# Two graph-attention layers on one core: h0's first pieces on POOL's queue, PSUM release by tile, another order at layer 2's opening and at its end

## The chip, the cores and the metric

The kernel runs on 1 core of one Trainium2 chip. The metric is the device time of that core in microseconds, the median of several runs. The core's engines are named as in the profile: PE (matrix products and transposes; PEld is its loading of weights), DVE and ACT (vector and scalar work), POOL (GpSimd, which here issues the gathers) and SP (which here issues plain loads and stores). SP, ACT and POOL each have a queue of DMA instructions that stands in the same row as the engine's other work; the transfers themselves run on the core's 16 DMA engines.

## The reference

A graph of 3125 nodes with 768 features has 53,125 edges, sorted by their destination: 25,000 random pairs in both directions and one loop for each node. The layer is two graph attentions with residual products:

```
h  = relu(layernorm(x))
h0 = h
h  = gat(h, W1, a_src1, a_dst1, b1, heads=4, out=256, concat)      # 1024 wide
h  = relu(layer_norm(h, g1, be1)) + (h0 @ Wr1 + br1)
h1 = h
h  = gat(h, W2, a_src2, a_dst2, b2, heads=1, out=768)
h  = layer_norm(h, g2, be2) + (h1 @ Wr2 + br2)
return x + h

gat: xl = x @ W
     e = leaky_relu(<xl[src], a_src> + <xl[dst], a_dst>, 0.2)
     alpha = exp(e - max over the edges of dst) / (sum over the edges of dst + 1e-16)
     out[dst] = sum over the edges of alpha * xl[src] + bias
```

Everything is float32.

## The kernel before

The nodes are cut into 25 blocks of 128 (the last, block 24, has 53). A block's edges lie in up to 17 tiles of 128 slots (8 in the last block), which are treated in five rounds (`ROUNDS`). Each tile is one gather: an indirect DMA on POOL's queue (lines 210 and 214) that reads 128 rows of a table in memory into a buffer `g`. PE then multiplies each gathered tile with a small matrix of weights into the block's accumulator `pa` in PSUM (line 782 in layer 1, 1437 in layer 2).

The stages follow each other in time. Up to about 300 us the kernel makes layer 1's table `h @ W1` and the lists of edges. From 300 to 490 us it looks up the scores of all edges and makes their weights `al`; beside this, `early` multiplies the first three groups of `h0` (`h0g`) with `Wr1` (line 1035, 24 products a group, each read out by ACT at line 1038 into `rt`). From 490 to 1183 us `sums` runs layer 1's gathers. It has 16 gather buffers, g0 to g15. Beside the sums, `later` makes the residual products that are left: it loads pieces of h0 (`h0k`, 11 buffers, line 1133), multiplies them into `pr` (line 190) and has ACT read them out (line 1157). The generator `first` calls `totals` once at the beginning: PE transposes the weights (line 599, tile `p` with the tag `p2`), ACT copies them out (line 601), DVE scans them into sums for each node (line 666), PE transposes back (line 610), SP stores the result `alo_d` (line 671), and POOL then looks up each block's own row of it (`ao`, line 724). At the end of each block `end1` does the layer norm, transposes, adds the residual, and multiplies with W2 into layer 2's table.

From 1183 us layer 2 runs: a ring of 36 gather buffers, the softmax of the edges of each block (`softmax`, in two parts of five transposes `mix` each, with DVE and ACT between), `summed` (the products into `pa`), `residuals` (a generator of 8 steps for each block, two products `pr` from a piece of h1 and `Wr2` each, called by `filled(n)`; after the 8th, DVE adds `pr` to `xr`, line 1329), and `finish` (own row, bias, layer norm, residual, store). While block b is summed, the softmax of block b + 1 is made. `STEPS` says how many residual steps follow each round, and `REST` how many come at a block's end:

```
AHEAD = 3
STEPS = [0, 1, 1, 0, 4]
REST = 2
```

The order on PE, ACT and DVE from 490 us on is that of the program's text (`tc.manual_schedule`); POOL and SP are ordered by the framework's scheduler. A pool of tiles gives its memory or its PSUM banks on in one of two ways: with `reuse_waits="tile"` a new tile waits for the readers of what lay in its own place, without it for the earlier pool as a whole. DMAs take their semaphores from two sets of eight, one for SP and ACT together and one for POOL; in a set, each DMA waits for the one that stood eight before it.

`own` is a block's own row of the table, which SP loads (line 227); `slots` holds the edge scores that `values` copies out of the gathered rows on ACT (line 1376); `load_own`, `own_share` and `store_rows` are helpers for the own row's load, its scaling with the share of the loop (on POOL, for the last block alone), and the store of the result. The source also has a second program for edges in any order, which does not run on this input.

Of the kernel before, what the change touches and what calls it, by code (L numbers as in the profile page):

```python
# [10 lines left out]
F32 = mybir.dt.float32  # L11
# [6 lines left out]
OP = mybir.AluOpType  # L18
AX = mybir.AxisListType
PSUM = bass.MemoryType.PSUM  # L20
# [49 lines left out]
def in_order(  # L70
# [16 lines left out]
    nc = tc.nc  # L87
# [4 lines left out]
    C2 = W2.shape[1]  # L92
    P = 128
# [132 lines left out]
        for o, e in pieces(b):  # L226
            q.dma_start(t[o:e], src_[b * P + o:b * P + e, :])

    def store_rows(q, dst_, b, t):
        for o, e in pieces(b):  # L230
            q.dma_start(dst_[b * P + o:b * P + e, :], t[o:e])

    def by_chunk(vec, pool, n, name):

# [564 lines left out]
    with tc.tile_pool(name="m1", bufs=1) as mp:  # L799
# [323 lines left out]

        with tc.tile_pool(name="w2", bufs=1, reuse_waits="tile") as wp, tc.tile_pool(name="e1", bufs=2, reuse_waits="tile") as ep, \
                tc.tile_pool(name="a1", bufs=1, reuse_waits="tile") as ap, \
                tc.tile_pool(name="g1", bufs=1, reuse_waits="tile") as gp, tc.tile_pool(name="pg1", bufs=1, space=PSUM) as pp:
            loaded, made, whole, gone = {}, {}, set(), set()

            def load(i, k, q=nc.sync):
                if i < NG:  # L1130
                    n = cols_of(i)
                    t = loaded[i, k] = wp.tile([128, WIDE], F32, name="h0k", bufs=11)
                    q.dma_start(t[:, :n], h0T_d[i][:, k, :n])

            for k in range(NK1):
                load(0, k, nc.scalar)
            b1_b = wp.tile([P, HC], F32, name="b1_b")
            nc.sync.dma_start(b1_b, bcast(b1, HC))
            def later():
# [102 lines left out]
    with tc.tile_pool(name="m2", bufs=1, reuse_waits="tile") as mp, \  # L1242
# [66 lines left out]
        def halves(t):  # L1309

            return t.rearrange("p (i n) -> p i n", i=2)
# [27 lines left out]
        def filled(n):  # L1339
            for _ in range(n):  # L1340
                next(fill, None)
# [24 lines left out]
        def load_own(b, cs=slice(0, C2)):  # L1366
            if b < NB:
                if b == NB - 1 and b not in owns:
                    owns[b] = small([128, NK2, P], "h1", bufs=3).rearrange("p k n -> p (k n)")[:, :C2]
                own = owns[b] = owns.get(b) or small([128, C2], "own")  # L1370
                load_rows(nc.sync, own[:, cs], table2[:, cs], b)
# [15 lines left out]
        def softmax(b):  # L1387

            nonlocal e0, w0
            at, pen = slots[b % 2], pens.pop(b)  # L1390
            mix = pp.tile([128, 1024], F32, name="mix")
            for c in range(WIN // 128):
                o = FROM[c % 4] + c // 4
                nc.tensor.transpose(mix[:, c * 128:(c + 1) * 128], at[:, o:o + 4].rearrange("p q n -> p (q n)"), ident)  # L1394
            top = small([P, 1], "top", bufs=2)
            e, e0 = e0 or small([P, WIN], "e"), None
            sums_ = mix[:, :WIN]
            nc.vector.tensor_tensor_reduce(out=sums_, in0=sums_, in1=pen, scale=1.0, scalar=-BIG,
                                           op0=OP.add, op1=OP.max, accum_out=top)
            nc.vector.tensor_scalar(top, top, both[:, b:b + 1], -1.0, op0=OP.max, op1=OP.mult)  # L1400
            nc.vector.scalar_tensor_tensor(top, top, SLOPE, top, op0=OP.mult, op1=OP.min)
            nc.scalar.activation(e, sums_, AF.Copy, scale=SLOPE)
            nc.vector.tensor_tensor(e, sums_, e, OP.max)
            v = small([P, 4], "v", bufs=3)
            nc.scalar.activation(e, e, AF.Exp, bias=top, accum_out=v[:, 0:1])
            nc.scalar.activation(v[:, 1:2], self_s[:, b:b + 1], AF.Exp, bias=top)
            penalty(b + 1)
            yield
            for c in range(WIN // 128):
                nc.tensor.transpose(mix[:, c * 128:(c + 1) * 128], e[:, c * 128:(c + 1) * 128], ident)  # L1410
            yield
            w, w0 = w0 or small([128, WIN], "w", bufs=2), None
            nc.vector.tensor_copy(w[:, :512], mix[:, :512])
            nc.scalar.activation(w[:, 512:], mix[:, 512:WIN], AF.Copy)
            shares[b] = w, v
# [26 lines left out]
        def finish(b, pa):  # L1442

            nonlocal z0
            r = rows_of(b)
            own, v = owns.pop(b), shares.pop(b)[1][:r]
            z, z0 = (z0 or small([P, C2], "z", bufs=2))[:r], None
            if b < NB - 1:
                p = pa[:, :, :f]
                nc.vector.scalar_tensor_tensor(p, halves(own), v[:, 2:3], p, op0=OP.mult, op1=OP.add)  # L1450
                yield
                nc.vector.scalar_tensor_tensor(p, p, v[:, 3:4], halves(b2_b), op0=OP.mult, op1=OP.add)
                yield from norm_steps(mp, p, C2, 1)
                mu, rstd = norm_steps.found
                nc.vector.scalar_tensor_tensor(p, p, mu, halves(g2_b), op0=OP.subtract, op1=OP.mult)
                nc.vector.scalar_tensor_tensor(halves(z), p, rstd, halves(xrs.pop(b)), op0=OP.mult, op1=OP.add)
            else:
                for i in range(2):
                    cs = slice(i * f, (i + 1) * f)
                    nc.vector.scalar_tensor_tensor(z[:, cs], pa[half_at(b, i), i, :f], v[:, 3:4], own[:r, cs],  # L1460
                                                   op0=OP.mult, op1=OP.add)
                yield
                yield from norm_steps(mp, z, C2, 1)
                mu, rstd = norm_steps.found
                nc.vector.scalar_tensor_tensor(z, z, mu, g2_b[:r], op0=OP.subtract, op1=OP.mult)
                nc.vector.scalar_tensor_tensor(z, z, rstd, xrs.pop(b)[:r], op0=OP.mult, op1=OP.add)
            store_rows(nc.scalar, out, b, z)

        def totals2(b):
            v = shares[b][1][:rows_of(b)]  # L1470
# [4 lines left out]
        def own_share(b):  # L1475
            r = rows_of(b)
            own, v = owns[b][:r], shares[b][1][:r]
            nc.gpsimd.tensor_scalar(own, own, v[:, 2:3], v[:, 3:4], op0=OP.mult, op1=OP.mult)
            nc.gpsimd.tensor_tensor(own, own, b2_b[:r], OP.add)

        with tc.manual_schedule(engines={PE, ACT, DVE}):
            penalty(0)
            fetch()
            load_own(0)
            filled(AHEAD * NK2)
            for k in range(len(ROUNDS)):
                values(0, k)
            made = softmax(0)
            next(made)
            filled(NK2 // 2)  # L1490
            next(made)
            next(made, None)
            totals2(0)
            values(1, 0)
            values(1, 1)
            ending = iter(())
            for b in range(NB):
                pa = pp.tile([P, 2, 512], F32, name="pa", bufs=2)
                opened = set()
                last = b + 1 == NB - 1  # L1500
                steps = STEPS if b else [0] * (len(ROUNDS) - 1) + [NK2 // 2 - REST]
                for k in range(len(ROUNDS)):
                    if last and k == 0:
                        load_own(b + 1)
                        for i in range(2, len(ROUNDS)):
                            values(b + 1, i)
                        made = softmax(b + 1)
                        next(made)
                    summed(b, k, pa, opened)
                    if k < 2:  # L1510
                        next(ending, None)
                        if 0 < b < NB - 1:
                            load_own(b, slice(k * f, (k + 1) * f))
                    if b + 1 < NB and not last:
                        if k < 3:
                            values(b + 1, k + 2)
                        if k == 2:
                            made = softmax(b + 1)
                            next(made)
                    if k == 2:  # L1520
                        for _ in ending:
                            pass
                    if k == 4:
                        ending = finish(b, pa)
                        next(ending)
                    if k == 4:
                        filled(steps[k])
                    if b + 1 < NB and k == (1 if last else 4):
                        next(made)
                        next(made, None)  # L1530
                        totals2(b + 1)
                        if last:
                            own_share(b + 1)
                    filled(REST if k == 4 else steps[k])
                if b + 2 < NB:
                    values(b + 2, 0)
                    values(b + 2, 1)
            for _ in ending:
                pass
# [472 lines left out]
```

## Time and profile before

| | |
|---|---|
| time, median of 3 runs | 1728.88 us (1728.3 to 1729.52) |
| the profiled execution | 1734.45 us, span 1732.3 us, mean granted clock 0.980 |
| busy share of the span | PE 94%, PEld 54%, DVE 58%, ACT 26%, POOL 50% |
| DMA | 546.69 MB, mean 316 GB/s |
| 0 to 300 us (table 1, lists) | PE busy 287.76 us, DMA share 0.55 |
| 300 to 490 us (weights of the edges) | PE busy 187.53 us, DMA share 0.44 |
| 490 to 1183 us (layer 1's sums) | PE busy 674.61 us, DMA share 0.98 |
| 1183 to 1732 us (layer 2) | PE busy 479.11 us, DMA share 0.98 |

The span is the stretch in which the profiled execution has records; its own time is 2.15 us longer. In a timeline, a row holds the start in us, the busy time, the engine ("ACTq" and "SPq" are DMA issues on those queues), the line, the operation, its output and inputs, the number of instructions, and in brackets the idle time ahead of it with what ended it. In a row of grouped instructions the count is followed by the busy time, the mean ns of one, and the idle time ahead of the group with its releasers. A DMA share of 1 means that all 16 engines are busy; it can read a little over 1.

### The profile page before, as it was taken

The numbers are of one execution on the slowest core, as the hardware profiler recorded it, in microseconds if no ns is written. First come the engines' busy times: TensorE is split into PE (matmuls) and PEld (weight loads), VectorE is DVE, ScalarE is ACT, GpSimd is POOL, SyncE is SP. The second block draws the span as 40 slices with busy tenths as digits, with TensorE's granted clock in tenths as the row PEclk, the third lists the DMA queues.
The fourth block names the chain that finished last, engine by engine and source line by source line (L and its number), as shares of the span: only waits on it lengthen the run. The fifth ranks groups of instructions, "written<-read, shape, count | busy, mean of one in ns | idle before, by whom it ended". The sixth has DMA issues, their size and how long they took to land.

```text
span 1732.3 us, 31368 instructions
## 1 busy us (share of the span) xinstructions
PE 1629.0 (94%) x11522; PEld 934.1 (54%) x11522; DVE 1004.0 (58%) x2604; ACT 456.0 (26%) x1312; POOL 871.9 (50%) x909
## 2 busy tenths in 40 slices
PE   7999999999979999999999999998799999998985
PEld 5666666566646556565565555544444444444431
DVE  6784343799963665565655656751344544444455
ACT  2122333100122122121221212112334444434443
POOL 2000010200055766667667666745777677777772
PEclk9999999999989999999999999999899999999997
DMA  6843546743189999999999999987999999999994
GB/s 225 278 135 117 144 119 183 275 141 121 45 300 346 408 403 396 404 395 404 406 391 408 387 378 384 410 340 276 385 378 396 378 395 396 393 397 396 380 350 161
DMA packets 188212, 546.69 MB, mean 316 GB/s; under 512 B 32072, under 2 KB 80072, under 8 KB 187922
## 3 DMA queue, kind: packets, MB, share of 16 engines
q0 software_dynamic: 99776, 387.46, 58.3%
q1 hardware_dynamic: 83880, 146.74, 24.3%
q10 hardware_dynamic: 4394, 10.39, 1.6%
q8 instruction: 94, 1.54, 0.4%
q14 instruction: 68, 0.56, 0.1%
HBM read 492.19 MB, written 65.62 MB: 322 GB/s over the span
## 4 chain that ended last, share of the span: by engine, by line
PE 69%; DMA 19%; DVE 7%; ACT 2%; issue 2%; SPq 1%; POOL 1%; POOLq 0%; ACTq 0%; DVEq 0%
PE pr L190 15%; PE p L190 14%; PE pm L190 13%; PE pa L782 11%; DMA g<-table,hi_s 6%; DMA g<-table,idx_s 6%; PE pa L1437 4%; PE pm L1035 4%; PE pq L580 3%; DMA h<-h1T_d 2%; DMA s<-slo_d 1%; PE mix L1394 1%; PE p L1200 1%; DMA xr<-in_x_dram 1%; DVE ab L504 1%
## 5 line engine op out<-in xcount | busy, mean ns | idle before, releaser
L210 POOL DMA_INDIRECT g<-table,idx_s x393 | 377.8, 961 | 324.4 <-DVE al L624 160.5
L214 POOL DMA_INDIRECT g<-table,hi_s x423 | 433.8, 1026 | 209.5 <-issue 92.9
L190 PE MATMUL pr<-wr,h 128*128 128x384 f32 x768 | 276.3, 506 | 7.8 <-issue 4.2
L190 PE MATMUL p<-w,h1T 128*128 128x384 f32 (+1 forms) x768 | 267.7, 496 | 0.0
L782 PE MATMUL pa<-g,w 128*32 128x256 f32 x3912 | 244.0, 383 | 7.9 <-DMA g<-table,hi_s 4.7
L190 PEld LDWEIGHTS pr<-wr,h 128*128 128x128 f32 x768 | 143.4, 196 | 117.7 <-issue 41.2
L190 PEld LDWEIGHTS p<-w,h1T 128*128 128x128 f32 x768 | 139.8, 189 | 113.0 <-issue 21.0
L782 PEld LDWEIGHTS pa<-g,w 128*32 128x32 f32 x3912 | 119.5, 110 | 125.8 <-issue 25.2
L1437 PE MATMUL pa<-g,w 128*32 128x384 f32 x1956 | 179.2, 505 | 0.8 <-DVE v L1471 0.8
L759 DVE TENSOR_TENSOR w<-oh,al 128x128 f32<-128x128 f32 (+1 forms) x416 | 132.0, 317 | 53.4 <-PE pa L782 28.7
L190 PE MATMUL pr<-h0k,wr 128*128 128x256 f32 (+1 forms) x576 | 143.2, 395 | 3.6 <-DMA h0k<-h0T_d 3.6
L190 PE MATMUL pm<-w,h0l 128*128 128x344 f32 x432 | 131.3, 459 | 2.0 <-ACT h0l L868 2.0
L190 PE MATMUL pm<-w,h0g 128*128 128x344 f32 x432 | 131.0, 458 | 0.3 <-ACT h0g L868 0.3
L1035 PE MATMUL pm<-h0g,wr 128*128 128x512 f32 x288 | 130.4, 599 | 0.0
L190 PEld LDWEIGHTS pr<-h0k,wr 128*128 128x128 f32 x576 | 106.2, 191 | 34.7 <-issue 11.1
L965 POOL DMA_DIRECT2D hot_d<-ohd x25 | 13.4, 535 | 213.1 <-DVE own L531 123.4
L1437 PEld LDWEIGHTS pa<-g,w 128*32 128x32 f32 x1956 | 58.1, 113 | 112.2 <-issue 97.8
L758 DVE TENSOR_SCALAR oh<-iota_f,rel_s 128x32 f32<-128x32 f32 (+1 forms) x416 | 113.1, 272 | 2.8 <-issue 2.7
L190 PEld LDWEIGHTS pm<-w,h0l 128*128 128x128 f32 x432 | 81.3, 192 | 42.3 <-ACT h0l L868 2.6
L190 PEld LDWEIGHTS pm<-w,h0g 128*128 128x128 f32 x432 | 81.3, 192 | 39.9 <-issue 1.2
L1233 DVE COPY asad<-p 128x2 f32<-128x2 f32 (+1 forms) x25 | 4.0, 159 | 155.2 <-ACT row L1231 155.2
L520 ACT ACTIVATE bn_sd<-bn_mv,eps 128x1 f32<-128x1 f32 (+1 forms) x50 | 14.7, 295 | 274.5 <-DVE bn_mv L516 269.7
(295 smaller groups left out, 1751.4 us busy)
## 6 DMA issues: line engine op xcount, KB each, us to landing
s<-slo_d SPq DMA_DIRECT2D x25, 544.0 KB
table<-row SPq DMA_DIRECT2D x24, 512.0 KB
own<-table SPq DMA_DIRECT2D x24, 512.0 KB
h1T_d<-h1T SPq DMA_DIRECT2D x24, 512.0 KB
h<-h1T_d SPq DMA_DIRECT2D x84, 128.0 KB
table<-row SPq DMA_DIRECT2D x24, 392.0 KB
ring<-in_x_dram SPq DMA_DIRECT2D x24, 384.0 KB
out_dram<-z ACTq DMA_DIRECT2D x24, 384.0 KB
```

What stands on the lines that cost most here:

```text
L190: nc.tensor.matmul(out_, lhsT, rhs, start=start, stop=stop)
L210: nc.gpsimd.indirect_dma_start(out=g, out_offset=None, in_=table[:, :], in_offset=bass.IndirectOffsetOnAxis(ap=idx_s[:, c], axis=0))
L214: nc.gpsimd.indirect_dma_start(out=g, out_offset=None, in_=table[:, :], in_offset=bass.IndirectOffsetOnAxis(ap=idx_k[:, c], axis=0), bound ...
L504: nc.vector.scalar_tensor_tensor(abs_[2 + m][:, cs], w[:, k, cs], 1.0, abs_[m][:, cs], op0=OP.mult, op1=OP.mult, accum_out=to[:, k, m * he ...
L580: nc.tensor.matmul(q[:, j], oh[:P, o:o + 128], tabs[:, i], start=(i == 0), stop=(i == 2))
L758: nc.vector.tensor_scalar(oh, iota_f[:, lo:hi], rel_s[:, c:c + 1], None, op0=OP.is_equal)
L759: nc.vector.tensor_tensor(w, oh[:, None, :].to_broadcast([128, heads, hi - lo]), al[:, POS[j], :, b:b + 1].to_broadcast([128, heads, hi - ...
L782: nc.tensor.matmul(pa[p0:p0 + 32, o // f, o % f:o % f + n], w[:, o // cols, :], g[:, o:o + n], start=to not in opened, stop=False, skip_gr ...
L1035: nc.tensor.matmul(pm, wr1[:, k, m * 128:(m + 1) * 128], groups[gi][:, k, :], start=(k == 0), stop=(k == NK1 - 1))
L1200: nc.tensor.transpose(pt[:, k, :r], z[:, (k0 + k) * 128:(k0 + k + 1) * 128], ident[:r, :r])
L1394: nc.tensor.transpose(mix[:, c * 128:(c + 1) * 128], at[:, o:o + 4].rearrange("p q n -> p (q n)"), ident)
L1437: nc.tensor.matmul(pa[p0:p0 + 32, i, :f], w_, g[:, i * f:(i + 1) * f], start=(i, q) not in opened, stop=False, skip_group_check=True)
```

## The change

There are five edits.

1. The first six pieces of h0 that `later` uses (`load(0, k, ...)`) are issued by POOL, where ACT issued them.
2. The PSUM pool of layer 1's sums (`pg1`) hands its banks on by tile, and two tiles, named `pr` and `p2`, are made first, so that these names get the first banks and `pa` the last four.
3. At layer 2's opening 23 residual steps are made instead of 24, then the whole softmax of block 0 without steps inside (before, four steps stood between its parts), then one step. Block 0 gets the same steps as the other blocks (8, where it had 4).
4. For block 23, the last full one, POOL scales the own row and adds the bias (`own_share(b)` after round 1), so that `finish` has one DVE operation ahead of the layer norm where it had two.
5. A block's store that is in pieces has its pieces after the first issued by SP; only the last block's store has a second piece (5 rows).

```
-    def store_rows(q, dst_, b, t):
+    def store_rows(q, dst_, b, t, q1=None):
         for o, e in pieces(b):
-            q.dma_start(dst_[b * P + o:b * P + e, :], t[o:e])
+            (q1 if q1 and o else q).dma_start(dst_[b * P + o:b * P + e, :], t[o:e])
...
-                ... tc.tile_pool(name="pg1", bufs=1, space=PSUM) as pp:
+                ... tc.tile_pool(name="pg1", bufs=1, space=PSUM, reuse_waits="tile") as pp:
...
+            for name in ("pr", "p2"):
+                pp.tile([128, 512], F32, name=name, bufs=2)
             for k in range(NK1):
-                load(0, k, nc.scalar)
+                load(0, k, nc.gpsimd)
...
-            if b < NB - 1:
+            if b == NB - 2:
+                p = pa[:, :, :f]
+                nc.vector.scalar_tensor_tensor(p, p, v[:, 3:4], halves(own), op0=OP.mult, op1=OP.add)
+                yield
+                yield from norm_steps(mp, p, C2, 1)
+                ...
+            elif b < NB - 1:
                 p = pa[:, :, :f]
                 nc.vector.scalar_tensor_tensor(p, halves(own), v[:, 2:3], p, op0=OP.mult, op1=OP.add)
                 yield
...
-            store_rows(nc.scalar, out, b, z)
+            store_rows(nc.scalar, out, b, z, nc.sync)
...
-            filled(AHEAD * NK2)
+            filled(AHEAD * NK2 - 1)
             for k in range(len(ROUNDS)):
                 values(0, k)
-            made = softmax(0)
-            next(made)
-            filled(NK2 // 2)
-            next(made)
-            next(made, None)
+            for _ in softmax(0):
+                pass
+            filled(1)
             totals2(0)
...
-                steps = STEPS if b else [0] * (len(ROUNDS) - 1) + [NK2 // 2 - REST]
...
+                        if last and k == 1:
+                            own_share(b)
...
-                        filled(steps[k])
+                        filled(STEPS[k])
...
-                    filled(REST if k == 4 else steps[k])
+                    filled(REST if k == 4 else STEPS[k])
```

On POOL's queue, where layer 1's first gathers start (`idx_s` holds the edges' row numbers; the names in brackets are the semaphores that a row waits for, DMASW1 being POOL's own set's second one, PE_49 a count of PE's), this stood before:

```order
L210 DMA g_4429<-table_64,idx_s 128x1024 [waits DMASW0_49]
L210 DMA g_4430<-table_64,idx_s 128x1024 [waits DMASW1_49]
L210 DMA g_4431<-table_64,idx_s 128x1024 [waits DMASW2_49]
L210 DMA g_4432<-table_64,idx_s 128x1024 [waits DMASW3_49]
L210 DMA g_4433<-table_64,idx_s 128x1024 [waits DMAHW4_49,DMAHW3_49,DMAHW7_49,DMASW4_49,Activation_49]
```

and this stands now:

```order
L210 DMA g_4431<-table_64,idx_s 128x1024 [waits DMASW0_49]
L1133 DMA h0k<-h0T_d 128x256 [waits DMASW1_49,PE_49]
L1133 DMA h0k<-h0T_d 128x256 [waits DMASW2_49,PE_49]
L1133 DMA h0k<-h0T_d 128x256 [waits DMASW3_49]
L1133 DMA h0k<-h0T_d 128x256 [waits DMASW4_49]
L1133 DMA h0k<-h0T_d 128x256 [waits DMASW5_49]
L1133 DMA h0k<-h0T_d 128x256 [waits DMASW6_49]
L210 DMA g_4432<-table_64,idx_s 128x1024 [waits DMASW7_49]
```

The six loads come after the fourth gather, and seven of the eleven gathers that stood in one row now stand behind them; the first two loads wait for a count of PE's. On ACT's queue the same place (the last copies of the weights' stage, then the copies of `totals`) held the loads before:

```order
L658 ACTIVATE scr<-eo 128x17x100
L1038 ACTIVATE rt<-pm,br_c 128x4x128
L1133 DMA h0k<-h0T_d 128x256 x6
L601 ACTIVATE scr<-p_4501 100x512
L601 ACTIVATE scr<-p_4507 100x512
L601 ACTIVATE scr<-p_4544 100x512
```

and no longer does:

```order
L658 ACTIVATE scr<-eo 128x17x100
L1038 ACTIVATE rt<-pm,br_c 128x4x128
L601 ACTIVATE scr<-p_4503 100x512
L601 ACTIVATE scr<-p_4509 100x512
L601 ACTIVATE scr<-p_4546 100x512
```

The copies follow the last read of `rt` directly. On PE, at layer 2's opening (`p` is layer 1's last product into table 2, `h` a block's h1), the order was:

```order
L194 MATMUL p_12134<-w_4742,h1T 21x386
L190 MATMUL pr<-wr_12203,h_12212 128x384 x16
L190 MATMUL pr<-wr_12203,h_12214 128x384 x16
L190 MATMUL pr<-wr_12203,h_12216 128x384 x16
L1394 MATMUL mix<-ident,slots_12189 128x128 x5
L190 MATMUL pr<-wr_12203,h_12330 128x384 x8
L1410 MATMUL mix<-ident,e 128x128 x5
L1437 MATMUL pa<-g_12242,w 32x384
```

and is now:

```order
L194 MATMUL p_12136<-w_4744,h1T 21x386
L190 MATMUL pr<-wr_12205,h_12214 128x384 x16
L190 MATMUL pr<-wr_12205,h_12216 128x384 x16
L190 MATMUL pr<-wr_12205,h_12218 128x384 x14
L1396 MATMUL mix<-ident,slots_12191 128x128 x5
L1412 MATMUL mix<-ident,e 128x128 x5
L190 MATMUL pr<-wr_12205,h_12218 128x384 x2
L1439 MATMUL pa<-g_12244,w 32x384
```

The four steps of block 3 (8 products) have left the place between the softmax's two parts, and the last step of block 2 (2 products) has moved behind it.

More of the change, by code (lines that the diff above doesn't have):

```diff
@@ L1125, in in_order @@
                 tc.tile_pool(name="a1", bufs=1, reuse_waits="tile") as ap, \
-                tc.tile_pool(name="g1", bufs=1, reuse_waits="tile") as gp, tc.tile_pool(name="pg1", bufs=1, space=PSUM) as pp:
+                tc.tile_pool(name="g1", bufs=1, reuse_waits="tile") as gp, tc.tile_pool(name="pg1", bufs=1, space=PSUM, reuse_waits="tile") as pp:
             loaded, made, whole, gone = {}, {}, set(), set()
@@ L1447, in finish @@
             z, z0 = (z0 or small([P, C2], "z", bufs=2))[:r], None
-            if b < NB - 1:
+            if b == NB - 2:
[3 more added lines that the diff above has]
+                yield from norm_steps(mp, p, C2, 1)
+                mu, rstd = norm_steps.found
+                nc.vector.scalar_tensor_tensor(p, p, mu, halves(g2_b), op0=OP.subtract, op1=OP.mult)
+                nc.vector.scalar_tensor_tensor(halves(z), p, rstd, halves(xrs.pop(b)), op0=OP.mult, op1=OP.add)
+            elif b < NB - 1:
                 p = pa[:, :, :f]
```

## Prediction

> **What bounds the kernel now.** I read the page first (span, busy shares, chain), then stretches, then the three places that the change touches in order of time.
>
> ```profile
> span 1732.3 us, 31368 instructions
> PE 69%; DMA 19%; DVE 7%; ACT 2%; issue 2%; SPq 1%; POOL 1%; POOLq 0%; ACTq 0%; DVEq 0%
> 490.00:515.00 25.00, 15.20 (x129) 10.12 (x130) 14.02 (x39) 3.78 (x9) 13.15 (x11) 0.80 0.98 357
> 515.00:536.00 21.00, 21.00 (x190) 15.48 (x192) 5.46 (x22) 4.90 (x14) 5.90 (x6) 0.99 0.72 252
> 536.00:563.00 27.00, 24.38 (x214) 15.20 (x204) 12.71 (x43) 5.11 (x14) 18.16 (x18) 1.00 1.03 399
> 563.00:1094.00 531.00, 530.50 (x4413) 309.61 (x4414) 326.41 (x1082) 109.42 (x310) 361.57 (x356) 1.00 1.02 397
> L210 POOL DMA_INDIRECT g<-table,idx_s x377 | 358.9, 952 | 155.1 <-issue 55.6 <-DMA hot<-hot_d 28.2 <-DMA g<-table,idx_s 21.0
> ```
>
> The chain is two thirds TensorE. The stretch rows give the busy us of PE, PEld, DVE, ACT and POOL, then granted clock, DMA share and GB/s. From 563 to 1094 (layer 1's gathers) PE is busy 530.5 of 531 us beside a full DMA: whatever PE gains before 563 goes through to layer 2's start, if DMA can deliver as much earlier. The one hole is 490 to 515, where PE works 15.2 of 25 us at clock 0.80. Layer 2 hangs on POOL instead: 377 gathers of 952 ns (the last row, 1183 to 1702 us) with some 0.30 us between them, 1.25 us each, are 472 us. So a shift of its start or a removed POOL stall counts fully there, and a faster PE alone counts nothing.
>
> **The opening of layer 1.**
>
> ```profile
> 489.01 0.83 ACTq L1133 DMA_DIRECT2D h0k<-h0T_d  x2
> 490.29 0.29 DVE L759 TENSOR_TENSOR w<-oh,al 128x128 f32<-128x128 f32 x1
> 490.75 2.24 PE L782 MATMUL pa<-g,w 128*32 128x256 f32 x32 [1.78 <-ACT rt L1038]
> ...
> 496.43 4.10 ACTq L1133 DMA_DIRECT2D h0k<-h0T_d  x4
> 500.62 1.09 ACT L601 ACTIVATE scr<-p 100x512 f32<-100x512 f32 x2 [9.92 <-DMA own<-table]
> 501.28 2.23 PE L599 MATMUL p<-ident,al 128*100 128x128 f32 x9 [5.41 <-ACT scr L601]
> 504.06 4.69 DVE L666 TENSOR_TENSOR_SCAN scr<-keep,scr 100x2176 f32<-100x2176 bf16 x1 [9.68 <-ACT scr L601]
> ...
> 510.34 0.70 PE L190 MATMUL pr<-h0k,wr 128*128 128x256 f32 x2 [2.30 <-DMA h0k<-h0T_d]
> 512.37 2.93 PE L190 MATMUL pr<-h0k,wr 128*128 128x256 f32 x6 [1.34 <-DMA h0k<-h0T_d]
> 515.09 1.09 PE L610 MATMUL p<-ident,scr 100*128 100x100 f32 x10
> 523.96 0.32 SPq L671 DMA_DIRECT2D alo_d<-scr  x1
> 531.16 0.96 POOL L724 DMA_INDIRECT ao<-alo_d,at_last  x1 [10.57 <-DMA alo_d<-scr]
> ```
>
> ACT's queue holds six loads of h0k. After two it stands 9.92 us until an unrelated load (own) has landed, and the copies L601 behind it wait: PE loses 5.41 us, the scan starts only at 504.06, and the products pr then lose 2.30 and 1.34 us because those loads land late. POOL stands 10.57 us for alo_d, which hangs on the scan.
>
> Moving the loads takes them off ACT. The release by tile lets pa start on its own banks: the 1.78 us wait for rt falls, but its fourth weight is made only at 490.58 (490.29 + 0.29), so I count 0.7. New order: pa to 492.3; eight transposes p (1.1) to 493.4; the second pa round (1.9) to 495.3; nine transposes p with ACT's copies behind them to 497.3. The scan runs 497.4 to 502.1. The third pa round and 16 records of pr (0.70 + 2.93 for 8 of them) end at 502.6, and L610 starts there instead of at 515.09: **12.5 us on PE**. That is the upper end.
>
> DMA sets the price that stays. From 490 to 563 it moved 357 x 25 + 252 x 21 + 399 x 27 = 25.0 MB; the six loads, 128 KB each, take 0.8 of it away. The rest at 399 GB/s needs 60.7 us of the 73: 12.3 us at most. By shares it is 0.98 x 25 + 0.72 x 21 + 1.03 x 27 = 67.4 us, at a full 1.03 65.5, less 2.0 for h0k: 63.5, a gain of 9.5. alo_d and ao move up by up to 12.5 us, but into a fuller DMA. I take 9.5, because some idle DMA will remain while alo_d is stored. The lower end is 2.4: six issues of some 0.4 us (0.83 for two) that ACT saves.
>
> What POOL pays:
>
> ```profile
> 432.45 0.69 ACT L1038 ACTIVATE rt<-pm,br_c 128x512 f32<-128x512 f32 x1 [6.76 <-PE pm L1035]
> 433.00:450.00 17.00, 17.00 (x177) 11.24 (x176) 15.83 (x22) 1.02 (x3) 0.00 (x0) 1.00 0.16 55
> 478.92 0.94 POOL L210 DMA_INDIRECT g<-table,idx_s  x1 [160.53 <-DVE al L624]
> 482.97 2.50 POOL L210 DMA_INDIRECT g<-table,idx_s  x1 [1.88 <-DVE m L653]
> ```
>
> POOL idles for 160.53 us ahead of 478.92. The six loads stand after the fourth of eleven early gathers and wait for PE: their tiles lie where the groups h0g0 and h0g1 stood, and the latter's last product is read out at 432.45 (the sixteenth of 24 such rows). So seven gathers move from about 310 to after 432, into a DMA that is 16% busy. At 1.25 us the 12 pieces left end near 448, at the 2.50 + 1.88 us seen beside a busy DVE near 485. I count nothing; the ends are 0.7 us gained (fewer transfers beside the lists' loads at 308) and 6 lost.
>
> The trace's slowest gather took 2.50 us beside fp32 work of DVE, the others 0.94. The Trainium skill (SBUF — State Buffer, SBUF: two separate sides) says that some VectorE operations lock GpSimd out of their shared SBUF ports, so that it cannot write descriptors, and advises issuing such loads from ACT or SP. That speaks against the move: by it, with 4.4 us for each of the 12, the term would be 3.5 instead of 9.5; the row shows it for one gather of five there.
>
> **The opening of layer 2.**
>
> ```profile
> 1213.06 0.58 ACT L1376 ACTIVATE slots<-g 128x32 f32<-128x32 f32 x4 [5.59 <-DMA g<-table,idx_s]
> 1215.55 0.71 PE L1394 MATMUL mix<-ident,slots 128*128 128x128 f32 x5
> 1216.75 0.96 DVE L1329 TENSOR_TENSOR xr<-pr,xr 128x768 f32<-128x768 f32 x1
> 1217.63 0.82 DVE L1398 CUSTOM_DVE_ANT_0 mix<-mix,pen 128x640 f32<-128x640 f32 x1
> 1219.87 8.04 PE L190 MATMUL pr<-wr,h 128*128 128x384 f32 x16 [3.61 <-DMA h<-h1T_d]
> 1220.56 0.83 ACT L1405 ACTIVATE e<-e,top 128x640 f32<-128x640 f32 x1
> 1229.24 4.08 PE L1437 MATMUL pa<-g,w 128*32 128x384 f32 x48 [0.78 <-DVE v L1471]
> ...
> 1231.46 0.95 POOL L210 DMA_INDIRECT g<-table,idx_s  x1 [1.77 <-ACT slots L1376]
> ...
> 1220.00:1225.00 5.00, 5.00 (x8) 2.70 (x9) 0.10 (x1) 3.20 (x6) 2.92 (x4) 0.50 1.03 390
> 1259.13 5.36 PE pr L190 x16
> ```
>
> Before, the softmax waits on DVE for block 2's additions (to 1217.71), and its second half on PE for four residual steps: those wait 3.61 us for h1 and then run at clock 0.50, 8.04 us instead of 5.36 (last row). After, one step fewer stands ahead (1.3 us), the values are there at 1213.64, so mix runs at 1214.4 and DVE starts at 1215.2. The 3.76 us from 1217.63 to the end of e at 1221.39 end at 1219.0; mix, the copy w (0.7 each) and one step bring pa to 1221.1, 8.1 us earlier. The four steps follow inside block 0 (5.4 us), so PE stays 2.7 us ahead. On PE's idle 3.8 us between the halves the clock may fall to 0.50, 4 us more for pa; its first gathers are free by 1226 still, ahead of 1229.99, when POOL wants them. What this is worth is POOL's stall there, 1.77 - 0.30 = **1.5 us**. The ends are 0 and 2.5 (another wait of POOL, 1.28 us at 1221.17, lies in the same crowd).
>
> **The tail.**
>
> ```profile
> 1684.61 20.92 SPq L227 DMA_DIRECT2D own<-table  x4
> 1713.19 0.99 POOL L1478 TENSOR_SCALAR h<-h,v 53x768 f32<-53x768 f32 x1 [11.92 <-DVE v L1473]
> 1714.27 1.82 POOL L1479 TENSOR_TENSOR h<-h,b_b 53x768 f32<-53x768 f32 x1
> 1715.95 1.02 DVE L1450 SCALAR_TENSOR_TENSOR pa<-own,v,pa 128x768 f32<-128x768 f32 x1 [0.83 <-PE pa L1437]
> 1717.01 1.03 DVE L1452 SCALAR_TENSOR_TENSOR pa<-pa,v,b_b 128x768 f32<-128x768 f32 x1
> 1726.80 0.95 ACTq L231 DMA_DIRECT2D out_dram<-z  x2
> ```
>
> For block 23 two DVE operations become one; from 1715.95 on everything is DVE's row, so 1.06 us go (1715.95 to 1717.01). POOL's pair (0.99 + 1.82) starts when own has landed: issued by 1705.5 and some 3 us on its way, it ends near 1711.5, 4.4 us before DVE needs it; the pair for block 24 starts at 1713.19 as before. If own came over 4.4 us later, each us would cost one. The last store's second piece is issued beside the first: half of 0.95, 0.5 us. Sum **1.5**, ends 0 and 1.6.
>
> **Sum.** 9.5 + 1.5 + 1.5 = 12.5 us. The profiled execution took 1734.45 us, 2.15 more than its span, and would take 1721.9. The median of the three runs is 1728.88, 5.6 below it; taken from that, 1716.4.
>
> **Rivals.**
> - *The DMA engines take it back.* DMA runs at 1.02 of full from 563 to 1094, so earlier requests may only queue longer. The page DMA: Bandwidth & Descriptors of the Trainium skill (Issuing engines are not separate DMA queues) says that another issuer saves only the issue time. Against it: the 9.92 us on ACT are a wait in the queue, not a transfer, and 28% of DMA lies idle from 515 to 536. With the lower end, 2.4 + 3.0: 1723.5.
> - *No difference.* Layer 1's end is set by its last gathers (DMA is at 1.02 until then), and the tail's 1.5 alone is left, with layer 2's 1.5 lost in later waits for PE: 1727.4.
> - *Slower: POOL is held too long.* If the loads are released only by the last product (PE free for pa at 490.75 at the latest) and not at 432, 12 pieces at 1.25 us and five gathers, 21 us, start at 490; the 16th gather leaves at 511 and lands some 12 us later, 523, where PE needed it before at about 516. That costs 7 us against before, and 3.0 come back: 1733. It decides from a release later than about 470. The rows speak for 432.
>
> **How the numbers follow.** Forecast, 9 to 17 us gained (the first term from 6 to 12.5 and the other ends): 0.62, range 1712 to 1720. DMA takes it back: 0.21, 1720 to 1725. No difference: 0.10. Slower: 0.07. What a measurement of this kernel can tell from no change is about 0.2%, 3.5 us. Faster by more than that: 0.83; within: 0.10; slower: 0.07. The range, 1711 to 1726, leaves out the slower case, most of no difference and a little at the lower end (12.5 + 2.5 + 1.6 is 16.6, 1712.3, and 0.7 from the lists).
>
> **What would show it.** Right: ACT's L601 directly behind PE's transposes, no wait of pr for h0k, the scan near 497, POOL's ao near 520, six loads of POOL after 432; layer 2's first gather some 9.5 us earlier; pa's first round near 1211 (that shift and 8 us); one DVE operation less between the last pa and the end. Wrong: PE's new waits for g between 530 and 560 as long as the gain (the first rival), POOL's first waiting load released near 488 (the slower one), or a longer POOL stall in block 0.

## The result and the profile after

The changed kernel took 1719.39 us (median of 6 runs, 1716.65 to 1721.48), the kernel before 1729.13 us (6 runs, 1728.3 to 1731.85). The ratio is 0.9939, with a 95% interval from 0.9925 to 0.9952: 8.3 to 13.0 us faster. The forecast was 1716.4, in a range from 1711 to 1726, and "faster" at 0.83. It held; how its terms came out is another matter.

The profiled execution after took 1719.44 us, as much as the median, while that of before (1734.45) stood 5.3 us above its median. So the two traces are 14.8 us apart, and not all of that is the change. From the page after, span and chain by engine:

```profile
span 1717.5 us, 31371 instructions
PE 77%; DMA 13%; DVE 4%; ACT 2%; issue 2%; POOL 1%; POOLq 0%; DVEq 0%; ACTq 0%
```

TensorE carries 77% of the chain where it carried 69%, DMA 13% where it carried 19%. The same stretches as before (busy us of PE, PEld, DVE, ACT, POOL; granted clock, DMA share, GB/s):

```profile
433.00:450.00 17.00, 17.00 (x174) 10.98 (x171) 14.96 (x20) 1.37 (x2) 7.86 (x9) 1.00 0.85 287
490.00:515.00 25.00, 24.75 (x227) 18.19 (x220) 15.86 (x43) 6.64 (x17) 17.19 (x13) 1.00 1.00 376
515.00:536.00 21.00, 19.52 (x180) 13.06 (x178) 11.05 (x39) 4.08 (x10) 11.53 (x12) 1.00 0.94 352
536.00:563.00 27.00, 23.15 (x179) 13.62 (x178) 12.45 (x40) 4.68 (x14) 15.79 (x17) 0.87 1.03 405
563.00:1094.00 531.00, 530.51 (x4389) 308.38 (x4389) 326.70 (x1088) 107.04 (x302) 360.66 (x356) 1.00 1.01 397
```

The hole from 490 to 515 is closed: PE works 24.75 of 25 us, where it worked 15.20. DMA is used at 433 (0.85, before 0.16). Part of the gain is given back from 515 to 563, where PE now has 5.3 us of holes (19.52 of 21 and 23.15 of 27) beside a nearly full DMA; before it had 2.6. The timeline of the opening:

```profile
430.89 1.63 POOL L1133 DMA_DIRECT2D h0k<-h0T_d  x3 [68.81 <-PE pm L1035]
442.06 0.94 POOL L210 DMA_INDIRECT g<-table,idx_s  x1 [0.30 <-issue]
487.43 3.31 PE L782 MATMUL pa<-g,w 128*32 128x256 f32 x32 [0.28 <-PE pm L1035]
491.35 1.09 ACT L601 ACTIVATE scr<-p 100x512 f32<-100x512 f32 x2 [2.46 <-PE p L599]
495.53 4.69 DVE L666 TENSOR_TENSOR_SCAN scr<-keep,scr 100x2176 f32<-100x2176 bf16 x1 [3.02 <-ACT scr L601]
497.04 3.72 PE L190 MATMUL pr<-h0k,wr 128*128 128x256 f32 x16
500.60 1.02 PE L610 MATMUL p<-ident,scr 100*128 100x100 f32 x10
521.12 0.96 POOL L724 DMA_INDIRECT ao<-alo_d,at_last  x1 [9.68 <-DMA alo_d<-scr]
533.21 1.89 PE L782 MATMUL pa<-g,w 128*32 128x256 f32 x26 [1.48 <-DMA g<-table,hi_s]
539.84 1.22 PE L190 MATMUL pr<-h0k,wr 128*128 128x256 f32 x2 [3.24 <-DMA h0k<-h0T_d]
540.99 3.64 PE L782 MATMUL pa<-g,w 128*32 128x256 f32 x32
559.81 2.53 PE L190 MATMUL p<-w,h1T 128*128 128x384 f32 x7
```

The last row is the first product into table 2, which began at 569.50 before. POOL's first load goes out alone at 361.49, the others when PE releases them at 430.89; the held gathers end at 443.0, ACT's copies follow PE's transposes, the scan stands at 495.53 and L610 at 500.60. Then PE waits for a gather (1.48 us) and for a later piece of h0 (3.24 us), behind which the clock has fallen: the 32 products pa at 540.99 take 3.64 us where 32 others take 1.93, and the granted clock is 0.50 from 541 to 545. Layer 2's opening and the end:

```profile
1211.97 1.33 PE L1412 MATMUL mix<-ident,e 128*128 128x128 f32 x5 [4.05 <-ACT e L1407]
1213.09 2.77 PE L190 MATMUL pr<-wr,h 128*128 128x384 f32 x4
1215.79 3.79 PE L1439 MATMUL pa<-g,w 128*32 128x384 f32 x32
1219.51 1.56 PE L190 MATMUL pr<-wr,h 128*128 128x384 f32 x4
1220.87 0.95 POOL L210 DMA_INDIRECT g<-table,idx_s  x1 [0.30 <-issue]
...
1694.54 0.99 POOL L1488 TENSOR_SCALAR own<-own,v 128x768 f32<-128x768 f32 x1 [6.39 <-DVE top L1400]
1702.17 1.03 DVE L1452 SCALAR_TENSOR_TENSOR pa<-pa,v,own 128x768 f32<-128x768 f32 x1 [0.59 <-PE pa L1439]
1711.97 0.29 SPq L231 DMA_DIRECT2D out_dram<-z  x1
1711.97 0.34 ACTq L231 DMA_DIRECT2D out_dram<-z  x1
```

The row at 1220.87 is POOL's 37th gather of the layer, which waited 1.77 us before and no longer does. Block 23's own share is scaled 4.7 us before DVE needs it (1694.54, 0.99 + 1.82 us of work, against 1702.17).

One table serves all that follows: the time between marks, each read from the start of a row in the trace ("p" is the first product p<-w,h1T, line 190; gathers are counted in layer 2). The kernels are the changed one and those of the experiments below that ran on chips of the same speed; the last two of these are given in the text.

| us between marks | before | after | after, again | loads by SP | all held | all held, 5 more | old opening 2 | no release by tile |
|---|---|---|---|---|---|---|---|---|
| first L1035 to first pa | 191.73 | 189.13 | 189.20 | 190.65 | 189.12 | 189.12 | 189.14 | 190.63 |
| first pa to L610 | 24.34 | 13.17 | 13.30 | 19.00 | 13.30 | 13.32 | 13.17 | 12.10 |
| L610 to p | 54.41 | 59.21 | 58.68 | 57.93 | 60.40 | 59.29 | 60.76 | 60.38 |
| p to gather 1 | 614.05 | 614.98 | 614.69 | 614.79 | 614.69 | 614.91 | 614.75 | 615.47 |
| gather 1 to 60 | 76.9 | 76.0 | 76.0 | 75.5 | 76.4 | 76.1 | 76.9 | 75.0 |
| gather 60 to 400 | 439.8 | 436.3 | 436.3 | 439.2 | 437.0 | 438.3 | 436.6 | 435.7 |
| gather 400 to the end | 32.0 | 30.4 | 30.5 | 30.7 | 31.5 | 30.7 | 31.1 | 30.2 |

How far may these numbers be trusted? Up to p, four traces are of the same code (after twice, old opening 2, and the run without block 23's share with 189.13, 13.30 and 59.20): their first two rows agree within 0.13 us, L610 to p within 2.1. From gather 60 to 400 it takes 435.4 (in that last run) to 439.2 us in kernels that are alike there. So a trace carries some 2 us of chance ahead of p and 3.8 in layer 2, and a part of the 14.8 us between the first two traces is of that kind.

### The profile page after: what moved, and what is told of

Its sections match the earlier page's. It is cut to its first block, busy times and chain, and to the rows that moved or that the text cites. A ratio compares the mean times of both kernels' runs of the same rounds, so it can differ in the third digit from the quotient of the medians.

```text
span 1717.5 us, 31371 instructions
## 1 busy us (share of the span) xinstructions
PE 1628.3 (95%) x11522; PEld 933.0 (54%) x11522; DVE 1004.6 (58%) x2603; ACT 454.9 (26%) x1312; POOL 879.3 (51%) x917
## 4 chain that ended last, share of the span: by engine, by line
PE 77%; DMA 13%; DVE 4%; ACT 2%; issue 2%; POOL 1%; POOLq 0%; DVEq 0%; ACTq 0%
PE pr L190 17%; PE p L190 15%; PE pm L190 13%; PE pa L782 12%; PE pm L1035 7%; DMA g<-table,hi_s 6%; DMA g<-table,idx_s 6%; PE pa L1439 4%; PE pq L580 3%; PE mix L1396 1%; PE p L1202 1%; ACT slots L1378 1%; DMA w<-in_L_gnn_W_dram 1%; PE pt L866 1%; DVE ab L504 1%
## 5 line engine op out<-in xcount | busy, mean ns | idle before, releaser
L1035 PE MATMUL pm<-h0g,wr 128*128 128x512 f32 x288 | 130.4, 599 | 0.0
```

The costliest lines, as they stand in the source:

```text
L1035: nc.tensor.matmul(pm, wr1[:, k, m * 128:(m + 1) * 128], groups[gi][:, k, :], start=(k == 0), stop=(k == NK1 - 1))
```

## The experiments

The first four runs were on a chip on which every kernel, before included, took 13% longer; they are compared with before on that chip only. The other eight were on two chips of the first speed (before 1730.4 and 1730.22 us).

**The kernel before, again.**

> The kernel before, unchanged, for a second trace. The two traces shown are 14.8 us apart and the medians 9.7, so one theory is that some 5 us of the first trace of before are of that execution alone; then this one has a span near 1727 us, and layer 2 (from its first gather, at 1183.55 us in the first trace, to the last at 1700.27, 516.7 us) takes 512 to 514 us. Rival: a profiled execution of this kernel always takes 5 us longer than the others; then the span is near 1732 again.

1955.84 us against 1955.52 for before on that chip, ratio 0.9997 (0.9976 to 1.0018). The question could not be answered here, since the chip differs: from the first to the last gather of layer 2 it took 703.0 us, not 516.7. Page of this run (slices of 2.5% of the span):

```profile
span 1956.0 us, 31368 instructions
GB/s 225 300 99 116 136 160 260 136 125 57 314 392 383 390 386 387 382 389 380 372 375 370 365 379 204 363 154 319 280 282 300 289 279 289 291 290 291 286 261 126
```

In layer 2 DMA moves 279 to 319 GB/s, in the first trace of before 378 to 397. Why is not known. It makes this chip a test of what happens where transfers are scarcer.

**Edits 1 and 2 alone.**

```
-load(0, k, nc.scalar)
+load(0, k, nc.gpsimd)        # and pg1: reuse_waits="tile", pr and p2 made first
```

> Edits 1 and 2 alone (the six loads of h0k by POOL, release by tile). My prediction's first term: 9.5 us, 1719.5 us. Reading of the two traces: 2.6 us from the weights' stage (the held gathers leave the DMA engines to the lists s<-slo_d), 6.4 us between the first pa and PE's product p near 560 us, 9.0 us in all. Rival, the DMA engines take it back: 2.4 us, 1727. In the trace the wait of DVE for s after 320 us should be gone (1.62 and 1.95 us before) and the first pa should stand near 488.

1946.96 us, ratio 0.9952 (0.9932 to 0.9973), some 9 us. The trace puts it elsewhere than I did. The opening's two stretches, in the row of stretches, first of before again on this chip, then of this kernel (first pa to L610, L610 to p):

```profile
494.11:517.58 23.47, 15.48 (x130) 10.38 (x130) 13.18 (x35) 3.07 (x7) 12.39 (x11) 0.82 1.00 366
517.58:578.62 61.04, 57.01 (x466) 37.01 (x464) 22.66 (x82) 12.51 (x34) 30.15 (x31) 0.93 0.92 347
```

```profile
488.02:503.71 15.69, 13.07 (x130) 8.16 (x130) 9.79 (x24) 4.45 (x9) 9.89 (x8) 1.00 0.97 336
503.71:572.79 69.08, 60.48 (x467) 36.83 (x465) 26.04 (x91) 12.38 (x34) 38.12 (x39) 0.90 0.96 365
```

7.8 us are won up to L610 and 8.0 lost again up to p, beside DMA shares of 0.92 to 1.00: in this stretch the prediction's first rival is simply true. From the first L1035 to the first pa it takes 190.67 us, against 198.14, 195.29 and 194.31 in the three kernels without these edits. That is more than on the other chips, and their own scatter is 3.8 us. The rest of the trace's gain, 2.3 us or more from p to the first gather (637.1, against 639.4 to 640.7) and 6.9 between the first and the last gather (696.1 against 703.0), is larger than the scatter of some 1 us that the other three have there. I have no account of it; the profiled execution was 4.5 us faster than this kernel's median.

**Edit 3 alone.**

```
-filled(AHEAD * NK2)          # ... four steps between the parts of softmax(0)
+filled(AHEAD * NK2 - 1)      # softmax(0) whole, then filled(1); block 0 with STEPS
```

> Edit 3 alone (layer 2's opening). Prediction: 1.5 us, one stall of POOL at its 37th gather (1.77 us before) gone, nothing else; 1727.5 us. Rival: nothing to measure, since stalls of POOL come back later in the layer. The two traces by themselves would give up to 4.3 us for layer 2 (POOL's stalls in excess of 0.30 us between the gathers fell), which I expect to be mostly of that one execution of before.

1956.39 us, ratio 1.0001 (0.9989 to 1.0013). On this chip POOL's 37th gather waited 29.17 us in any case, since its buffer's product came late. No gain here says little about the other chips.

**Edits 4 and 5 alone.**

> Edits 4 and 5 alone (block 23's own share by POOL, the second piece of the last store by SP). Prediction: 1.5 us, 1.06 of it from the DVE operation and 0.5 from the store; 1727.5 us. Rival: the own row lands so late that DVE waits for POOL: 0. In the trace, from the last pa of block 23 to the end, 1.0 to 1.6 us less than the 16.4 of before (1715.95 to 1732.3).

1952.77 us, ratio 0.9992 (0.9977 to 1.0006). From the last pa of block 23 (counted from DVE's first operation behind it) to the end it takes 15.30 us, against 16.58 to 16.66 in the three others: 1.3 us, in the forecast's span, too little for the time to tell.

**The changed kernel, again.**

> The changed kernel itself, as the control of the next three. 0.994 of before on a chip like that of the prediction (9.7 us), 0.9945 if the chip is like the slower one of the first four runs (the parts there: 8.6 us for edits 1 and 2, 0 for edit 3, 1.6 to 2.7 for 4 and 5).

1717.69 us, ratio 0.9936 (0.9919 to 0.9954). The marks agree with the first trace of after to 0.6 us everywhere.

**The loads by SP.**

```
-load(0, k, nc.gpsimd)
+load(0, k, nc.sync)          # everything else as changed
```

> The changed kernel with h0's six first pieces issued by SP, not POOL: ACT is as free as after the change, but POOL's first eleven gathers are no longer held behind the loads and go out near 304 to 318 us, as before. Theory H (some 3 to 7 us of the gain come from the held gathers, which leave the DMA engines to the lists s): from the first product L1035 to the first pa 192 to 198 us instead of 189 to 191, and 3 to 6 us slower than the changed kernel. Rival O, the prediction's own account (the gain comes from ACT's freed copies alone, the early part is 0): equal to the changed kernel within 1 us, or faster by up to 1.

1725.18 us, ratio 0.9976 (0.9965 to 0.9986), which does not touch the 0.9936 above: some 7 us lost. Its timeline at the opening:

```profile
489.42 3.75 SPq L1133 DMA_DIRECT2D h0k<-h0T_d  x6
493.53 4.69 DVE L666 TENSOR_TENSOR_SCAN scr<-keep,scr 100x2176 f32<-100x2176 bf16 x1 [3.02 <-ACT scr L601]
496.72 0.70 PE L190 MATMUL pr<-h0k,wr 128*128 128x256 f32 x2 [0.80 <-DMA h0k<-h0T_d]
498.64 0.70 PE L190 MATMUL pr<-h0k,wr 128*128 128x256 f32 x2 [1.23 <-DMA h0k<-h0T_d]
500.32 4.27 PE L190 MATMUL pr<-h0k,wr 128*128 128x256 f32 x10 [0.97 <-DMA h0k<-h0T_d]
504.43 1.02 PE L610 MATMUL p<-ident,scr 100*128 100x100 f32 x10
```

ACT is free and the scan stands 8.1 us after the first pa, as in the changed kernel. But SP issues the loads at 489, into a full DMA; they land late, PE stands three times on pr, which is ahead of L610 in its order, and L610 comes 19.00 us after the first pa, not 13.30. So what the freed ACT queue gives by itself is small: together with the release by tile 2.9 us up to p (270.48 before, 267.58 here, the sum of the first three rows of the table). Another 4.5 to 6.4 (263.07 to 261.18 in the four traces named above) come when POOL sends the loads. Of these 1.45 us are theory H's: without held gathers the first pa comes 190.65 us after L1035, not 189.20, and DVE waits 7.8 us for the lists s, as before. The rest, 3.0 to 5.0 us behind the first pa, comes from the moment at which the loads go out; both theories missed this larger part. The split holds in this order only: no run has the loads early and ACT still held up.

The Trainium skill (DMA: Bandwidth & Descriptors, Issuing engines are not separate DMA queues) would have another issuer save only the time of issuing; that may hold of the transfer itself, but these 7 us hang on when the issuer comes to the load. The Trainium skill (SBUF — State Buffer, SBUF: two separate sides) advises ACT or SP rather than POOL for a DMA beside certain VectorE operations; followed for these six loads, it loses the 7 us, and three of POOL's issues at 430.89 took only 1.63 us beside a DVE that was busy 1.66 of the 2.11 us up to 433.

**All eleven gathers held.**

```
+with tc.issue_after(held[-1].ins):     # held: the six loads' instructions
     gather(g, table, b, j, turn < ahead)
```

> The changed kernel, with all eleven early gathers put behind the six loads (in the changed kernel four go ahead of them). Theory H: the last wait of DVE for s (4.19 us at 316) goes too, the first pa comes 2 to 4 us earlier, 2 to 4 us faster than the changed kernel. Rival: by 432 us DVE has caught up or the gathers are now late for pa, 0 to 2 us slower.

1718.49 us, ratio 0.9932 (0.9915 to 0.9949): no difference from the changed kernel. What DVE waited for in the weights' stage (us in total, times, longest), in before, after and here:

```profile
DVE ohs L548 <- DMA s<-slo_d: 7.8, 3, 4.2
```

```profile
DVE ohs L548 <- DMA s<-slo_d: 4.2, 1, 4.2
```

```profile
DVE ohs L550 <- DMA s<-slo_d: 0.8, 1, 0.8
```

The wait is gone, and the first pa comes 189.12 us after L1035, as before this edit. The last 3.4 us were covered by other work; theory H pays to 1.45 us and no further.

**Five more pieces early.**

```
+for k in range(5):
+    load(1, k, nc.gpsimd)              # beside the edit above
```

> As the one before, and the next five pieces of h0 also issued by POOL behind the first six (at about 435 us, DMA then 16% busy in the trace of before) and not by SP at 494, in the full stretch. If bytes in the stretch from 490 to 560 set what PE gets there, 0.64 MB less at 400 GB/s: another 1.6 us. Rival: PE's waits there hang on the order of the requests, not on the bytes: 0.

1720.15 us, ratio 0.9943 (0.9927 to 0.9959). The 0.64 MB moved out of the full stretch bring no gain that shows: 72.6 us from the first pa to p, against 73.7 in the run before it and 72.4 and 72.0 in the changed kernel. The 1.6 us that bytes would give lie within the scatter of 2 us, so this run does not settle whether bytes set the price. PE now stands here:

```profile
PE pr L190 <- DMA h0k<-h0T_d: 4.4, 1, 4.4
```

That is one wait, like the 3.24 us of after. The 11 buffers are now all filled early, so it is for a piece that can only be loaded once one of them has come free; fewer bytes in the stretch did not spare PE this wait.

**Edit 3 undone.**

> The changed kernel with layer 2's old opening (edit 3 undone, the others kept). Prediction: 1.5 us slower than the changed kernel, POOL's wait ahead of the 37th gather (1.77 us before, 0.30 in both traces of the changed kernel) back, the first pa 45 to 46 us after the first gather instead of 40.5 to 41.0. Rival from the slower chip, where edit 3 alone gave a ratio of 1.0001: no difference, since other waits of POOL for PE at later block ends grow or shrink by as much. By the two first traces it could be up to 4.4 us (first to last gather 516.7 before, 512.4 in both traces of the changed kernel).

1720.49 us, ratio 0.9938 (0.9915 to 0.9962). The 37th gather waits again, and the first pa stands 45.75 us after the first gather:

```profile
1224.62 0.95 POOL L210 DMA_INDIRECT g<-table,idx_s  x1 [1.07 <-ACT slots L1378]
```

From gather 1 to 60 it takes 76.9 us, as before; the traces with the edit in the table take 75.0 to 76.4. So the edit gives about 1 us there (0.5 to 1.9), and the scatter from gather 60 on (435.4 to 439.2) buries it.

**Edit 2 undone.**

> The changed kernel without edit 2 (the pool pg1 as before). Prediction: 0.7 of the 1.78 us that PE waited for rt come back, later steps of the opening move with it, 0.5 to 1.1 us slower in the trace up to L610, and less at PE's product p, where the stretch is bound by DMA; 0 to 1 us in the time. Rival: the first pa is the step on which all else hangs (the second pa round, the scan): 1.8 us or more.

1719.0 us, ratio 0.9935 (0.9913 to 0.9957), no difference that the time shows. In the trace the first pa starts 1.4 us later (190.63 after L1035, not 189.20), but its 32 products take less:

```profile
486.38 2.24 PE L782 MATMUL pa<-g,w 128*32 128x256 f32 x32 [1.79 <-ACT rt L1038]
```

With the release by tile they take 3.31 us, because PE starts on them while DVE is still making their weights w (three waits of some 0.3 us for w from 487 to 489 in after, none here). At the end of this round 0.4 us of the 1.4 are left, at L610 0.2 to 0.4 (202.73 us after L1035, against 202.30 and 202.50). At p, 263.11 us after L1035, it is within the scatter of the changed kernel (261.18 to 263.07).

**Edit 4 undone.**

> The changed kernel with edit 4 undone and edit 5 kept. If edit 5 brings 0.5 us as predicted, from the last pa of block 23 to the end 15.8 to 15.9 us; if it brings nothing (what the two traces say: 16.35 before, 15.33 after, and 1.06 of the difference is the DVE operation), 16.3 to 16.4. Time 1.0 us above the changed kernel in both.

1718.78 us, ratio 0.9941 (0.9918 to 0.9964). From the last pa of block 23 to the end 16.43 us, with the store's second piece issued by SP in the same instant as the first; before 16.35, after 15.33 and 15.29. So the DVE operation is 1.1 us and the split store 0.

**37 gather buffers.**

```
-RING = 36        small([128, 224], "room")
+RING = 37        small([128, 64], "room")
```

> The changed kernel with 37 gather buffers in layer 2, not 36 (its room made by a pad of 640 bytes less). It tests what the prediction says of layer 2, that POOL's cadence and its waits for a free buffer set the time. If so, the waits of POOL for PE at gathers 53, 233, 282, 331 and 380 (0.8 to 2.6 us each) become up to 1.25 us shorter each: 2 to 6 us faster than the changed kernel. Rival: the DMA engines (share 0.98 in layer 2) set it; POOL's waits get shorter, but the gathers land no earlier: 0 to 1 us.

1731.57 us, ratio 1.0010 (0.9997 to 1.0023): 12 to 14 us slower than the changed kernel, which neither the expectation nor its rival had. The reason is in the opening:

```profile
1168.69 4.36 POOL L1281 DMA_DIRECT2D wr<-in_L_gnn_Wr_dram  x8 [33.25 <-PE p L194]
1186.02 2.29 PE L190 MATMUL pr<-wr,h 128*128 128x384 f32 x3 [17.65 <-DMA h<-h1T_d]
```

The pad seems to have placed the weights Wr2 on memory that comes free early (in the changed kernel these loads go out near 1140 us); here they wait for PE's last product of layer 1, and the first residual steps wait 17.65 us behind them (none in after, where they start at 1171.09). Gathers 1 to 60 take 84.8 us. From gather 60 to 400 it takes 434.4, the least of all traces, and POOL's waits at gathers 282, 331 and 380 are below 0.45 us. That is in the direction of the prediction's account of layer 2, but 1.0 to 1.3 us below the best of the others is too close to the scatter to count as shown.

No version beat the changed kernel beyond the scatter.

## Why the prediction was right, and where its terms were not

**The sum.** Forecast 12.5 us; measured 9.7 us by the two medians, 10.5 by the first ratio (0.0061 of 1729) and 11.1 by the second. By the marks, the opening of layer 1 with the stage ahead of it is worth 7.4 to 9.3 us up to p (270.48 less 263.07 to 261.18), layer 2's opening about 1, the end 1.1. The forecast's 9.5, 1.5 and 1.5 lie a little above each.

**The first term came out near by luck: two errors cancel in part.** The step "DMA sets the price that stays" gave 9.5, in which 0.7 were for the earlier pa. Measured are 4.8 to 6.8 from the first pa to p (78.75 less 73.93 to 71.98), and 2.5 to 2.6 ahead of the first pa. The chain to L610 was right: 12.5 us forecast for PE there, of which 0.7 ahead of the first pa, 11.0 to 11.2 measured behind it. What failed is the price: 4.3 to 6.4 us were given back between L610 and p (54.41 before, 58.68 to 60.76 after), not 3.0, in waits for gathers and for a piece of h0, and in the first trace also in the clock that fell behind one of them. The account by bytes and shares did not see these waits; whether fewer bytes would lower the price stays open. On the slower chip all that was won up to L610 was given back by p.

**"I count nothing" for the early part was wrong.** The bounds were 0.7 gained to 6 lost. The held gathers gave 1.1 (the kernel without release by tile, 190.63 against 191.73) to 1.45 us (held or not, with release), because DVE's wait for the lists s at 320 to 332 us fell away: 3.6 us less wait, of which less than half shows. None of the 6 us was lost: the twelve pieces had gone out by 443 us, not 448 or 485. The text had called 2.50 us the trace's slowest gather and the others 0.94; that was misread, since the next two took 1.66 and 1.53 and one at 506.39 took 3.16. The release by tile let the first pa start 1.4 us earlier (1.1 without held gathers), but only 0.4 were left at the end of that round, less than the 0.7 forecast.

**The reason I gave for the gain was the smaller one.** The prediction's view went to ACT's 9.92 us in its queue. That wait did disappear, but the run with the loads on SP, where it disappears too, keeps only 2.9 us up to p, edit 2 included. The larger part is that the loads land before PE wants them, and that the gathers are held. The text had that as the 2.30 and 1.34 us which pr lost; it did not see that PE, in order, would stand on pr ahead of L610 as soon as the scan is early.

**Layer 2's opening.** The stall of 1.77 us at the 37th gather went, as said. "pa's first round near 1211" was 4.8 us off (1215.79). The first mix transposes came 2.3 us later than reckoned (1207.20, where 1214.4 less 9.5 is 1204.9): layer 2's first gather moved by 8.76 us, not 9.5, and behind it mix stood no earlier than before (32.4 us, before 32.0). Most of the rest is the clock: the second mix transposes took 1.33 us after 4.05 us of idle PE (0.71 before), and four products 2.77 us, where the next four took 1.56; the granted clock is 0.51 from 1211 to 1218. The text had counted 4 us for that as possible. The Trainium skill (TensorE: Matmul & The Clock Gate, Part 1: The HAM clock gate) gives about 3.4 us without work as what halves the clock; the row with 4.05 us agrees. In layer 1's opening a wait of 3.24 us was already followed by a clock of 0.50, one of 2.60 us in the second trace of after was not (1.00). The 1.5 us shrank to about 1, below what the time can tell.

**The end.** The DVE operation gave 1.1 us (1.06 forecast), the split store nothing of its 0.5. That the end follows the first, larger piece would explain it; no run shows that by itself.

**The rivals.** "The DMA engines take it back" is in part true on the first chips (4.3 to 6.4 of some 11 us) and wholly on the slower one, for that stretch. "POOL is held too long" did not occur: the second load was released at 430.89, which the prediction read as 432 from the product that it waits for. "No difference" is true of edits 2, 3 and 4, each undone by itself, and of 4 and 5 together on the slower chip, as far as the time can tell. Its mechanism, that layer 1's later gathers keep what the opening wins, did not occur: from p to gather 1 it takes 614.05 us before and 614.5 to 615.5 after (with 36 buffers).

## What to carry to other kernels

A load that moves to another queue is worth what its new moment of issue is worth: ask first when that queue comes to it, how full the DMA engines are then, and which engine stands in order on what it brings. The same six loads, taken off the same busy engine, were worth 7 us more on the queue that reached them 58 us earlier. Two terms that come out near their sum are no proof of either; marks at the ends of the stretches, in several traces, show which part each has, and how large the chance is in a part that nothing has changed.

## What the runs showed of the hardware

A gather that POOL begins during DVE's scan ends only after the scan. In the changed kernel's second trace, and in before (shown above: scan 504.06, 4.69 us):

```profile
493.62 4.69 DVE L666 TENSOR_TENSOR_SCAN scr<-keep,scr 100x2176 f32<-100x2176 bf16 x1 [3.02 <-ACT scr L601]
493.88 5.23 POOL L214 DMA_INDIRECT g<-table,hi_s  x1 [0.30 <-issue]
```

```profile
506.39 3.16 POOL L214 DMA_INDIRECT g<-table,hi_s  x1 [3.32 <-PE pa L782]
```

Both end 0.80 us after the scan (499.11 against 498.31, and 509.55 against 508.75), where a gather alone takes 0.99 us; after's first trace has the same 5.23 us. So the scan, one step from which all of the opening hangs, costs POOL up to 4.2 us of issue as well. The Trainium skill (SBUF — State Buffer, SBUF: two separate sides) describes an exclusive lock of shared ports, by which certain VectorE operations keep GpSimd from writing descriptors until they end. The traces fit that, with the end 0.80 us behind the scan's; the page does not name the scan, and no run here shows the lock itself. It was no danger to the held gathers at 433 to 443 us: beside a DVE that was busy 14.96 of 17 us they took 0.94 to 1.39 us each.
